# Perceiver block on one core: due times, a load queue and buffer places between attention and FFN

## The chip, the core and the metric

One core of a Trainium2 chip runs the whole program. The metric is device time in microseconds of one execution, as the median of several runs; smaller is better. The engines are named as in the profile: PE is the matrix engine (PEld its weight load), DVE the vector engine, ACT the scalar engine, POOL is GpSimd, SP only issues transfers (SPq its queue).

## What is computed

Four sequences of 128 tokens with 1024 features go through cross attention over four contexts of 2048 tokens (all 8192 context tokens are keys for all queries, with quantised q, k, v and attention), causal self attention with rotary positions, and an FFN whose weights are 4-bit:

```python
x = x + xattn(layernorm(x), ctx, Wq, bq, Wkv, bkv, Wp, bp)     # ... @ Wp + bp
x = x + attn(layernorm(x), Wq, bq, Wk, bk, Wv, bv, Wo, bo)     # ... @ Wo + bo
x = x + ffn(layernorm(x), gate_up_packed, gate_up_scales, down_packed, down_scales)
# ffn: h = silu(x @ Wg.T) * (x @ Wu.T);  y = h @ Wd.T;  y / sqrt(mean(y*y) + 1e-6)
```

## The kernel before

**Split products.** Precise products are made of three passes of a rounded 32-bit type. `split` (L155 to L159) makes of a tensor a high part on ACT (`split_hi`, L155) and on DVE a low part and a difference (`split_lo`, L158 and L159). A product accumulates high times high and low times low into one PSUM tile `acc_a`, and difference times difference into `acc_b`; two DVE operations join them (L1111, L1112). Before it is used, the low part of the activations is scaled on ACT (`scale_low`, L1087).

**The stretch of the change.** After the cross attention the work between attention and FFN is cut into ten halves, `PARTS`, numbered h = 0 to 9: the two column halves of the cross attention's projection Wp (0, 1), the first half of V (2), Q and K halves (3 to 6), the second half of V (7), and the two halves of Wo (8, 9). Each half runs over the four sequences t = 0 to 3, and each of these over eight k-steps of 128 features (`product_step`, L1100; three matmuls of 512 columns a step). Half 0 is a plain product, with its own matmuls (`first_step`, L941) on transposed chunks xoT.

**Weights.** Each half's weights come in four pairs kp = 0 to 3 of 512 KB. `load_pair` (L1028) transfers one into one of two buffers `w_raw`, `split_pair_hi` is its ACT part and `split_pair` its DVE part (tiles sw_h, sw_l, sw_d, six of each). A load waits for the split of the pair two before it. A half's bias goes by `load_bias` (L1018) as a row broadcast to 128 partitions; `add_row` (L1042) adds the row of a projection to the residual x1 on POOL.

**The norm.** After the second half of a projection, for each sequence: join into x1 (`join_residual`), `stats` (L1126), `normalise` (L1131 to L1137, with a root on ACT, L1134) to a tile xn, then `xn_transposes`: eight transposes on PE (L1080), from whose PSUM tiles `pt` (three buffers) the split goes to x3 (tiles x_h, x_l, x_d). Half 1 ends so before V, half 9 before the FFN. For half 1, sequence t's operands come from `first_split` (L1064, L1065) and `first_difference` (L1072), made during half 0.

**Order.** Inside `manual_schedule` the order is written by hand: `do(time, function, ...)` puts a step on an agenda whose times are counted in k-steps, and `perform` records all steps sorted by time (by order of entry where times are equal). Each engine then runs its own instructions in that order, and waits where an operand or buffer is not there. A half starts at `s = PART * h` with PART = 32; sequence t of it ends at `e = s + 8 * t + 8`. Before, the transposes of a norm are due at

```python
do(e + 0.4, normalise, t)
do(e + 7.5, xn_transposes, t)
do(e + 8.35, scale_low, t)
```

The first gate and up product (`first_gate_up`, L1253) is due 12 steps after half 9 and ends the hand order.

**FFN.** There a scheduler orders the instructions. `load_ffn` (L1378) loads 512 KB of weights into one of two buffers fw_raw on SP and splits them (fw_h, fw_l, fw_d); 21 further gate and up pairs follow, then 22 down products. The FFN's tiles take the place of tiles of the stretch before, and an instruction that writes one waits for the last use of whatever lay there. Pools are placed one after the other in the order in which they are opened.

Of the kernel before, what the change touches and what calls it, by code (L numbers as in the profile page):

```python
# [34 lines left out]
F32 = mybir.dt.float32  # L35
# [4 lines left out]
F32R = mybir.dt.float32r  # L40
# [6 lines left out]
P = 128  # L47
B, S, C = 4, 128, 1024
# [23 lines left out]
NI = INNER // P  # L72
# [4 lines left out]
EARLY = 8  # L77
# [9 lines left out]
def tile_perceiver(  # L87
# [26 lines left out]
    nc = tc.nc  # L114
# [29 lines left out]
    def split(src, hi, lo, df):  # L144

        split_hi(src, hi)
        split_lo(src, hi, lo, df)
# [66 lines left out]
    def do(step, fn, *args):  # L219
        agenda.append((step, len(agenda), fn, args))  # L220
# [230 lines left out]
    for t, at in enumerate((4, 10.5, 20, 22.6)):  # L451
# [3 lines left out]
        for n in range(2):  # L455
            at = (10 + 8.15 * t, 42.6 + 7.05 * t)[n]
# [16 lines left out]
    at = 70.8  # L473
# [166 lines left out]
    for s in range(V_AUTO, 2 * KT):  # L640
        at = TILE * s
# [8 lines left out]
    at = TILE * V_AUTO  # L650
# [5 lines left out]
    for s in range(V_AUTO, KT - 2):  # L656
        e = TILE * (s + 1)
# [4 lines left out]
    at = TILE * (KT - 2)  # L662
# [5 lines left out]
    at = TILE * KT  # L668
# [12 lines left out]
    for u in range(KT):  # L681
        at = TILE * (KT + u)
        s = KT + u
# [14 lines left out]
    at = TILE * (KT + 2)  # L698
# [6 lines left out]
    for u in range(first, last):  # L705
        at = TILE * (KT + u)
# [5 lines left out]
    at = TILE * (2 * KT - 1)  # L712
# [21 lines left out]
    with tc.tile_pool(name="at_e", bufs=1) as at_e, tc.tile_pool(  # L734
        name="at_s", bufs=4
    ) as small, tc.tile_pool(name="at", bufs=2) as at, tc.tile_pool(
        name="at_ps", bufs=3, space=PSUM
# [219 lines left out]
        with tc.manual_schedule():  # L957
            for s in range(n_steps + LAG_V):
                n, g = divmod(s, NSC)
# [9 lines left out]
                if n < len(units):  # L969
                    h, t = units[n]  # L970
# [44 lines left out]

    def load_bias(b, n):
        row = sa.tile([P, 512], F32, name="row", tag="row", bufs=3)
        nc.sync.dma_start(out=row, in_=b[ts(n, 512)].partition_broadcast(P))  # L1018
        return row

    def load_pair(h, kp):

        raw = sa_f.tile([P, 2, 512], F32, name="w_raw", tag="w_raw", bufs=2)
        if h < len(PARTS):
            src = w_src2[h][:, 2 * kp : 2 * kp + 2, :]
        else:
            src = gu_d[kp].rearrange("p (two k) n -> p two (k n)", two=2)
        nc.sync.dma_start(out=raw, in_=src)  # L1028
        live["raw", h, kp] = raw

    def split_pair_hi(h, kp):
# [9 lines left out]
    def add_row(t, n, row):  # L1041
        nc.gpsimd.tensor_tensor(x1[:, t, ts(n, 512)], x1[:, t, ts(n, 512)], row, ALU.add)  # L1042
# [107 lines left out]
    def join_values(h, t, n, row):  # L1150
        join(h, t, row[0], vs[n][:, t, :])
# [123 lines left out]
    with tc.manual_schedule():  # L1275
        do(-10, make_causal_mask, nc, mask, -1e30)
        do(-10, last_chunks)
        for step in early_steps[len(FIRST_AT) :]:
            do(-9.4, first_step, *step)
        for n in range(2):  # L1280
            do(-10, keep, ("bp", n), load_bias, xbp, n)
            for t in range(NT):
                do((-9, 15.5)[t // 2] + 8 * n, lambda t, n: add_row(t, n, rows["bp", n]), t, n)
        do(15.4, live["load_x"], 1)

        for h, (w, n) in enumerate(PARTS):
            s = PART * h

            if h > 0:
                for kp in range(NC // 2):  # L1290
                    at = s + {1: (-28, -22, -16, -10), 2: (-37, -33, -6, -3)}.get(h, (-26, -16, -6, -3))[kp]
                    do(at - 9.5, load_pair, h, kp)
                    do(at - 2.5, split_pair_hi, h, kp)
                    do(at + 0.5, split_pair, h, kp)
            if h == 1:
                do(0.6, lambda: nc.sync.dma_start(out=cs, in_=rope.rearrange("i p d -> p i d")))
            bias = {2: abv, 3: abq, 4: abk, 5: abq, 6: abk, 7: abv}.get(h)
            if bias is not None:
                do(s + (-20 if h < 5 else 8 * (17, 21, 25)[h - 5] - s), keep, h, load_bias, bias, n)
            if h in (3, 5):  # L1300
                m = (h - 3) // 2
                do(s + 8, keep, ("bo", m), load_bias, abo, m)
                for t in range(NT):
                    do(s + 9, lambda t, m: add_row(t, m, rows["bo", m]), t, m)
            if h in (2, 7):
                do(s, half_tile, vs, "v", n, f"x{n}")
            for t in range(NT):
                g = s + GROUP * t
                e = g + GROUP
                for k in range(NC):  # L1310
                    if h > 0:
                        do(g + k, product_step, h, t, k)
                    elif t > 1 or k == NC - 1:
                        do(g + k if t > 1 else 14 + t, first_step, t, k)
                if h == 0:
                    if t < 2:
                        e = 15 + t
                        do(14.2 + t, first_split, t)
                    else:
                        do(-9.5 if t == 2 else g - 4.5, first_transposes, t)  # L1320
                        do(g + 1.5, first_split, t)
                    do(PART + (0.05, 3, 9, 15)[t], first_difference, t)
                    do(e + 0.2, join_residual, h, t, n)
                    do(e + 0.3, stats, t, 0)
                elif h == 1:
                    do(e + 0.2, join_residual, h, t, n)
                    do(e + 0.3, stats, t, 1)
                    do(e + 0.4, normalise, t)
                    do(e + 7.5, xn_transposes, t)
                    do(e + 8.35, scale_low, t)  # L1330
                elif h in (2, 7):
                    do(e + 0.2, lambda *a: join_values(*a, [rows[a[0]]]), h, t, n)
                elif h in (3, 5):
                    do(e + 0.2, lambda *a: join_rotary(*a, [rows[a[0]]]), h, t)
                    do(e + 6.5, rotary_transposes, h, t, "qT", 4)
                elif h in (4, 6):
                    do(e + 0.2, lambda *a: join_rotary(*a, [rows[a[0]]]), h, t)
                    do(e + 6.5, rotary_transposes, h, t, "kT", 2)
                    do(e + 9.5, causal_scores, t, n)
                    do(e + 16.6, causal_exponentials, t, n)  # L1340
                    v = e + 24 if n == 0 else e + PART + 2
                    if n == 0 and t == 0:
                        do(v, half_tile, aos, "ao", n, "x2")
                    if n == 1 and t == 0:
                        do(v, half_tile, aos, "ao", n, "x0")
                    for q in range(2):
                        do(v + 0.5 + 2 * q, causal_transposes, t, n, q)
                        do(v + 3.5 + 2 * q, causal_values, t, n, q)
                    if n == 1:
                        do(v + 10.5, ao_transposes, t)  # L1350
                        do(v + 13, scale_low, t)
                else:
                    do(e + 0.2, join_residual, h, t, n)
                    do(e + 0.3, stats, t, n)
                    if n == 1:
                        do(e + 0.4, normalise, t, FP4_UP)
                        do(e + 7.5, xn_transposes, t, True)
                        do(e + 8.35, scale_low, t)
        s = PART * len(PARTS)
        for i in range(2):  # L1360
            at = s - 26 + 10 * i
            do(at - 9.5, load_pair, len(PARTS), i)
            do(at - 2.5, split_pair_hi, len(PARTS), i)
            do(at + 0.5, split_pair, len(PARTS), i)
        do(s + 12, first_gate_up)
        perform()
# [1 line left out]
    opool_s.close()  # L1368


    with tc.tile_pool(name="ff_t", bufs=2) as ff_t, tc.tile_pool(name="ff", bufs=1) as ff:
        hT = [ff.tile([P, 512], F32, name=f"hT{j}", tag=f"hT{j}") for j in range(NI)]
        ss = ff.tile([P, NT, 2], F32, name="ss")

        def load_ffn(src, n):

            raw = ff_t.tile([P, C], F32, name="fw_raw", tag="fw_raw")
            nc.sync.dma_start(out=raw.rearrange("p (i n) -> p i n", n=n), in_=src)  # L1378
            parts = [ff_t.tile([P, C], F32R, name=f"fw_{c}", tag=f"fw_{c}") for c in "hld"]
            split(raw, *parts)  # L1380
            return [t.rearrange("p (i n) -> p i n", n=n) for t in parts]
# [15 lines left out]
        def split_inner(pool, j):  # L1397
            hi, lo = (pool.tile([P, 512], F32R, name=f"h3_{c}{j}") for c in "hl")
            nc.scalar.mul(hi, hT[j], 1.0 - 0.5 / UP)
            nc.vector.tensor_tensor(lo, hT[j], hi, ALU.subtract)  # L1400
            nc.vector.tensor_scalar_mul(lo, lo, UP)
            df = ff.tile([P, 512], F32R, name=f"h3_d{j}", tag=f"hT{j}")
            nc.vector.tensor_tensor(df, hi, lo, ALU.subtract)
            h3[j] = [hi, lo, df]

# [30 lines left out]
        with tc.tile_pool(name="ff_h", bufs=1) as ff_h, tc.tile_pool(  # L1436
            name="y_ps", bufs=1, space=PSUM
# [113 lines left out]
```

## Time and profile before

| | |
|---|---|
| median of 3 runs | 2880.05 us (2878.3 to 2881.0) |
| the profiled execution | 2883.89 us, span 2882.1 us |
| mean granted clock | 0.979 |
| busy, share of the span | PE 93%, DVE 84%, ACT 44%, POOL 16% |
| keys and values, then cross attention | 0 to about 2160 us |
| projection, self attention, Wo (halves 0 to 9) | about 2160 to 2490 us |
| FFN | from about 2490 us |

Times in the profile are microseconds from the span's start. A line of the timeline has start, duration, engine, line, operation, output and inputs, count, and in brackets how long the engine was idle before it and what ended that. "issue" stands where the profile shows no other engine as the cause. A granted clock below 1.00 means that PE ran part of the time at a lower rate. A row of the table of stretches covers the time that its first column names.

### The profile page before, as it was taken

How to read it: one execution, taken by the hardware profiler on the slowest of the kernel's cores; microseconds unless marked ns; L12 is line 12 of the kernel's file. 1: busy time of each engine (PE TensorE's matmuls, PEld its weight loads, DVE VectorE, ACT ScalarE, POOL GpSimd, SP SyncE). 2: the span in 40 equal slices, each digit the busy share in tenths (PEclk: the TensorE clock that was granted, in tenths of full speed). 3: DMA queues.
4: the chain of work that ended last, by engine and by line, in shares of the span. 5: the costliest groups of instructions: out<-in, count | busy, mean ns of one | idle time of the engine just before them, and what ended most of it. 6: DMA issues, size and time to landing. Idle time of an engine off the chain costs nothing.

```text
span 2882.1 us, 41034 instructions
## 1 busy us (share of the span) xinstructions
PE 2666.1 (93%) x15480; PEld 2067.8 (72%) x15480; DVE 2418.6 (84%) x3959; ACT 1266.1 (44%) x1399; POOL 454.6 (16%) x608
## 2 busy tenths in 40 slices
PE   8999999999999999999987877787778899799998
PEld 3788888888888888888864555555555777688876
DVE  6899999555799989898879999999986898676674
ACT  4211212121323333333219999999983245333332
POOL 0011111000012222222122233322311000000000
PEclk9999999999999999999998999999999999899999
DMA  5555565222348777777437788878882322122222
GB/s 186 168 198 199 199 211 211 95 95 95 135 125 205 193 191 186 192 181 198 108 87 162 143 167 163 170 161 154 159 167 87 95 70 67 52 95 92 92 91 91
DMA packets 452711, 413.17 MB, mean 143 GB/s; under 512 B 356953, under 2 KB 361625, under 8 KB 452513
## 3 DMA queue, kind: packets, MB, share of 16 engines
q1 hardware_dynamic: 404928, 252.22, 36.6%
q0 software_dynamic: 46528, 157.29, 17.2%
q8 instruction: 121, 1.98, 0.3%
q10 hardware_dynamic: 1056, 1.05, 0.2%
q14 instruction: 78, 0.63, 0.1%
HBM read 220.14 MB, written 104.34 MB: 113 GB/s over the span
## 4 chain that ended last, share of the span: by engine, by line
PE 71%; DVE 20%; issue 4%; POOL 2%; ACT 1%; DMA 1%; SPq 0%; DVEq 0%; ACTq 0%; POOLq 0%
PE kv_a L342 33%; PE kv_b L342 16%; DVE e L787 13%; PE acc_a L1100 3%; PE y_a L1454 3%; PE gate_a L165 3%; PE up_a L165 3%; POOL sk L760 2%; PE acc_b L1100 2%; PE y_b L1454 1%; PE gate_b L165 1%; PE up_b L165 1%; PE q_ps L292 1%; PE a_pt L830 1%; PE sc L780 1%
## 5 line engine op out<-in xcount | busy, mean ns | idle before, releaser
L342 PE MATMUL kv_a<-w_h,c_h 128*128 128x512 f32 x2048 | 806.3, 394 | 0.0
L342 PE MATMUL kv_a<-w_l,c_l 128*128 128x512 f32 x2048 | 806.0, 394 | 0.2 <-ACT w_l L246 0.2
L342 PE MATMUL kv_b<-w_d,c_d 128*128 128x512 f32 x2048 | 806.0, 394 | 0.0
L787 DVE CUSTOM_DVE_ANT_0 e<-sc,sk 128x1024 f32<-128x1024 f32 x512 | 593.2, 1219 | 8.8 <-PE sc L780 7.7
L815 ACT ACTIVATE a<-e,m,sqs 128x4096 int16<-128x4096 f32 x128 | 486.9, 3804 | 25.2 <-DVE m L804 24.8
L342 PEld LDWEIGHTS kv_a<-w_l,c_l 128*128 128x128 f32 x2048 | 384.8, 188 | 89.6 <-ACT w_l L246 0.6
L342 PEld LDWEIGHTS kv_a<-w_h,c_h 128*128 128x128 f32 x2048 | 384.9, 188 | 88.9 <-issue 0.2
L342 PEld LDWEIGHTS kv_b<-w_d,c_d 128*128 128x128 f32 x2048 | 384.8, 188 | 88.9 <-DVE c_d L159 0.3
L155 ACT ACTIVATE c_h<-c_raw 128x1024 fp32r<-128x1024 f32 x128 | 135.1, 1057 | 415.8 <-PE kv_a L342 413.5
L356 DVE SCALAR_TENSOR_TENSOR f<-kv_a,bkv 128x512 f32<-128x512 f32 x256 | 175.6, 686 | 163.3 <-PE kv_a L342 162.6
L780 PE MATMUL sc<-kt,qT 64*128 64x512 bf16 x1024 | 207.4, 397 | 102.5 <-DVE mx L787 98.5
L581 ACT CAST kst<-kT 128x512 bf16<-128x512 int16 x128 | 89.4, 698 | 309.0 <-DMA kT<-ki 309.0
L830 PE MATMUL a_pt<-ident,a 128*128 128x128 f32 x1024 | 176.5, 297 | 20.7 <-ACT a L815 16.1
L357 DVE SCALAR_TENSOR_TENSOR f<-kv_b,f 128x512 f32<-128x512 f32 x256 | 176.6, 690 | 20.3 <-DVE f L356 0.9
L760 POOL PARTITION_BROADCAST sk<-sk_row x120 | 142.5, 1297 | 312.9 <-DVE mx L787 312.7
L830 PEld LDWEIGHTS a_pt<-ident,a 128*128 128x128 f32 x1024 | 113.0, 146 | 87.2 <-ACT a L815 48.6
L780 PEld LDWEIGHTS <-qT 64*128 64x128 bf16 x1024 | 74.8, 93 | 130.9 <-issue 101.2
L158 DVE TENSOR_TENSOR fw_l<-fw_raw,fw_h 128x1024 fp32r<-128x1024 f32 x64 | 78.2, 1223 | 107.1 <-ACT fw_h L155 106.9
L158 DVE TENSOR_TENSOR c_l<-c_raw,c_h 128x1024 fp32r<-128x1024 f32 x128 | 155.6, 1215 | 6.2 <-ACT c_h L155 5.9
L159 DVE SCALAR_TENSOR_TENSOR c_d<-c_l,c_raw 128x1024 fp32r<-128x1024 f32 x128 | 156.2, 1220 | 2.3
L155 ACT ACTIVATE fw_h<-fw_raw 128x1024 fp32r<-128x1024 f32 x64 | 67.8, 1061 | 179.7 <-PE y_a L1454 75.1
L548 ACT CAST vq<-vi 128x1024 f16<-128x1024 int16 x64 | 66.9, 1046 | 174.2 <-DVE vi L541 128.8
(203 smaller groups left out, 4114.1 us busy)
## 6 DMA issues: line engine op xcount, KB each, us to landing
c_raw<-in_ctxT SPq DMA_DIRECT2D x128, 512.0 KB, 3.6
v_d<-f POOLq DMA_DIRECT2D x64, 512.0 KB, 3.1
vl<-v_d POOLq DMA_DIRECT2D x64, 512.0 KB, 4.2
gu_d<-w_ffn POOLq DMA_DIRECT2D x44, 512.0 KB, 3.1
fw_raw<-gu_d SPq DMA_DIRECT2D x42, 512.0 KB, 3.4
k_d<-kst POOLq DMA_DIRECT2D x128, 128.0 KB, 3.5
vq_d<-vq POOLq DMA_DIRECT2D x32, 512.0 KB, 5.3
kt<-k_d SPq DMA_DIRECT2D x64, 256.0 KB, 3.6
```

Source lines behind the costliest of these rows:

```text
L155: nc.scalar.mul(hi, src, 1.0 - 0.5 / UP)
L158: nc.vector.tensor_tensor(lo, src, hi, ALU.subtract)
L159: nc.vector.scalar_tensor_tensor(df, lo, -1.0 - UP, src, ALU.mult, ALU.add)
L165: nc.tensor.matmul(ps, lhsT=lhs(i, k), rhs=rhs(i, k), start=(k == 0 and i != 1), stop=(k == NC - 1 and i != 0),)
L342: nc.tensor.matmul(ps, lhsT=tokens[s][i][:, k, :], rhs=w3[s < KT][k][i][:, ts(n, 512)], start=(k == 0 and i != 1), stop=(k == NC - 1 and i ...
L356: nc.vector.scalar_tensor_tensor(f, a, 1.0 + 1.0 / UP, bias[s < KT][n], ALU.mult, ALU.add)
L357: nc.vector.scalar_tensor_tensor(f, b, -1.0 / UP, f, ALU.mult, ALU.add)
L760: nc.gpsimd.partition_broadcast(tile_of_scales(h, g), sks_at[h][32 * c : 32 * c + 1, ts(half, SC)], channels=P)
L780: nc.tensor.matmul(ps[:, ts(i, 512)], lhsT=qT[rows, h, ts(t, P)], rhs=kts[h, g // 2][rows, ts(g % 2, 512)], start=True, stop=True,)
L787: nc.vector.tensor_tensor_reduce(out=state[n]["e"][-1][:, ts(g % (NSC // NEC), SC)], in0=ps, in1=sks_at[h, g], scale=1.0, scalar=LOWEST, o ...
L815: nc.scalar.activation(a, st["e"][c], AF.Exp, bias=st["m"], scale=sqs[:, 0, t, h : h + 1], accum_out=sums[h][:, t, c : c + 1],)
L830: nc.tensor.transpose(pt[:, i, :], a[:, at_word + P * i : at_word + P * i + P], ident)
```

## The change

It changes four things, and no operation. First, due times: the transposes after half 1 go from e + 7.5 to e + 9.5, behind two k-steps of the next sequence; after half 9 they go to e + 9.5 for sequences 0 and 1, e + 8.6 for 2, and stay for 3, so that the norm of sequence 3 comes ahead of the split of sequence 2. Second, the weight pairs of half 1 get other due times. Third, the two rows of the bias bp and the pairs 0 and 1 of half 1 are issued on GpSimd's queue instead of SP's. Fourth, the FFN's raw buffers get a pool of their own, behind a new pool of the first ten hT tiles, so that fw_raw lies where bias rows and an xn buffer were (before, it lay where values of the attention were), and fw_h, fw_l and fw_d move down by 8 KB a partition.

```diff
     def load_bias(b, n):
         row = sa.tile([P, 512], F32, name="row", tag="row", bufs=3)
-        nc.sync.dma_start(out=row, in_=b[ts(n, 512)].partition_broadcast(P))
+        queue = nc.gpsimd if b is xbp else nc.sync
+        queue.dma_start(out=row, in_=b[ts(n, 512)].partition_broadcast(P))
...
     def load_pair(h, kp):
...
-        nc.sync.dma_start(out=raw, in_=src)
+        queue = nc.gpsimd if (h, kp // 2) == (1, 0) else nc.sync
+        queue.dma_start(out=raw, in_=src)
...
-                    at = s + {1: (-28, -22, -16, -10), 2: (-37, -33, -6, -3)}.get(h, (-26, -16, -6, -3))[kp]
+                    at = s + {1: (-28, -24, -12, -7), 2: (-37, -31, -6, -3)}.get(h, (-26, -16, -6, -3))[kp]
                     do(at - 9.5, load_pair, h, kp)
                     do(at - 2.5, split_pair_hi, h, kp)
                     do(at + 0.5, split_pair, h, kp)
...
                     do(e + 0.4, normalise, t)
-                    do(e + 7.5, xn_transposes, t)
-                    do(e + 8.35, scale_low, t)
+                    do(e + 9.5, xn_transposes, t)
+                    do(e + 10.4, scale_low, t)
...
                         do(e + 0.4, normalise, t, FP4_UP)
-                        do(e + 7.5, xn_transposes, t, True)
-                        do(e + 8.35, scale_low, t)
+                        do(e + (9.5, 9.5, 8.6, 7.5)[t], xn_transposes, t, True)
+                        do(e + (10.4, 10.4, 8.7, 8.35)[t], scale_low, t)
...
-    with tc.tile_pool(name="ff_t", bufs=2) as ff_t, tc.tile_pool(name="ff", bufs=1) as ff:
-        hT = [ff.tile([P, 512], F32, name=f"hT{j}", tag=f"hT{j}") for j in range(NI)]
+    with tc.tile_pool(name="ff_t", bufs=2) as ff_t, tc.tile_pool(
+        name="ff_a", bufs=1
+    ) as ff_a, tc.tile_pool(name="ff_raw", bufs=2) as ff_raw, tc.tile_pool(name="ff", bufs=1) as ff:
+        inner_pool = [ff_a if j < EARLY + 2 else ff for j in range(NI)]
+        hT = [inner_pool[j].tile([P, 512], F32, name=f"hT{j}", tag=f"hT{j}") for j in range(NI)]
...
         def load_ffn(src, n):
-            raw = ff_t.tile([P, C], F32, name="fw_raw", tag="fw_raw")
+            raw = ff_raw.tile([P, C], F32, name="fw_raw", tag="fw_raw")
...
-            df = ff.tile([P, 512], F32R, name=f"h3_d{j}", tag=f"hT{j}")
+            df = inner_pool[j].tile([P, 512], F32R, name=f"h3_d{j}", tag=f"hT{j}")
```

## The prediction

> **What bounds the kernel now.** I read the table of stretches first, then the waits of TensorE, then the timelines of the three places where it stands. Columns of the stretches: busy time of PE, PEld, DVE, ACT and POOL (instructions in brackets), granted clock, DMA share, GB/s.
>
> ```profile
> 2155.00:2160.00 5.00, 4.10 (x58) 2.86 (x53) 1.63 (x4) 0.00 (x0) 0.00 (x0) 1.00 1.12 322
> 2160.00:2165.00 5.00, 4.11 (x54) 2.62 (x55) 0.59 (x2) 0.00 (x0) 0.00 (x0) 1.00 1.05 241
> ...
> 2174.00:2212.00 38.00, 28.25 (x76) 15.87 (x75) 27.89 (x30) 14.48 (x16) 6.83 (x5) 0.82 0.36 117
> 2212.00:2264.00 52.00, 44.73 (x196) 35.87 (x195) 40.37 (x58) 15.33 (x21) 0.00 (x0) 0.93 0.16 47
> ...
> 2452.00:2509.00 57.00, 41.81 (x179) 33.22 (x178) 37.92 (x59) 16.95 (x24) 0.00 (x0) 0.85 0.17 56
> 2509.00:2690.00 181.00, 181.00 (x777) 145.61 (x778) 126.87 (x151) 65.64 (x90) 0.00 (x0) 1.00 0.28 90
> ```
>
> The FFN (last row) keeps PE busy throughout, so nothing is to be won there. In the 147 us of the three stretches that the change touches, PE stands 32 us and its clock falls to 0.82 to 0.93.
>
> Place A, the first output projection (timelines of ACT, DVE, PE and the SP queue):
>
> ```profile
> 2119.96 40.57 SPq L845 DMA_TRANSPOSE aT_d<-a  x8
> 2160.88 0.81 SPq L1018 DMA_DIRECT2D row<-in_xbp  x2
> ...
> 2176.54 1.06 ACT L155 ACTIVATE sw_h<-w_raw 128x1024 fp32r<-128x1024 f32 x1 [5.75 <-DMA w_raw<-in_xWp]
> 2177.50 1.04 ACT L155 ACTIVATE x_h<-x 128x1024 fp32r<-128x1024 f32 x1
> 2179.72 0.68 DVE L1117 TENSOR_TENSOR x<-acc_a,x 128x512 f32<-128x512 f32 x1
> 2180.50 5.38 PE L941 MATMUL acc_a<-wp,xoT 128*128 128x512 f32 x8 [5.54 <-issue]
> ```
>
> ACT waits 5.75 us for the third weight pair with the x_h of sequence 0, which needs nothing from it, queued behind. DVE's join (L1117) comes behind that, and PE waits for the accumulator that the join frees. Place B is the norm of half 1, place C that of half 9 and the door of the FFN:
>
> ```profile
> 2205.22 3.78 PE L1100 MATMUL acc_b<-sw_d,x_d 128*128 128x512 f32 x8 [4.21 <-DVE x_d L1072]
> 2242.74 1.94 PE L1080 MATMUL pt<-ident,xn 128*128 128x128 f32 x8 [4.68 <-DVE xn L1137]
> 2484.03 1.95 PE L1080 MATMUL pt<-ident,xn 128*128 128x128 f32 x8 [6.01 <-DVE xn L1137]
> 2492.44 1.95 PE L1080 MATMUL pt<-ident,xn 128*128 128x128 f32 x8 [6.46 <-DVE xn L1137]
> ...
> 2478.34 1.23 DVE L158 TENSOR_TENSOR fw_l<-fw_raw,fw_h 128x1024 fp32r<-128x1024 f32 x1
> 2479.60 1.17 DVE L158 TENSOR_TENSOR fw_l<-fw_raw,fw_h 128x1024 fp32r<-128x1024 f32 x1
> 2480.75 1.22 DVE L159 SCALAR_TENSOR_TENSOR fw_d<-fw_l,fw_raw 128x1024 fp32r<-128x1024 f32 x1
> 2481.95 1.21 DVE L159 SCALAR_TENSOR_TENSOR fw_d<-fw_l,fw_raw 128x1024 fp32r<-128x1024 f32 x1
> 2483.08 0.81 DVE L1137 TENSOR_SCALAR xn<-x,ln_mv,ln_rstd 128x1024 f32<-128x1024 f32 x1
> ```
>
> PE waits for the normalised xn, and at C DVE spends 4.8 us on splits of FFN weights in the middle of the norm of sequence 2. After a stand over 4 us the eight transposes take 1.95 us instead of 1.05: each long gap costs a slow clock on top.
>
> **The change part by part.** No instruction is added or removed; what changes is order, queue and addresses. The sum is made against the profiled execution (2883.89 us, span 2882.1, 1.8 us around it), which lies 3.84 us above the median of 2880.05.
>
> *Place A, order.* With the new due times ACT splits the third pair after the x_h of sequences 0, 1 and 2. ACT ends the first two sw_h at 2170.8, so x_h of sequence 0 no longer waits; DVE is busy with the two first splits until 2174.95 (2169.87 and four ops), then x_l and the join: 2174.95 + 1.15 + 0.7 = 2176.8 against 2180.4, 3.6 us earlier. But a new wait comes: DVE has the x_l of sequence 3 ahead of the fourth pair's split, and its x_h stands on ACT behind the sw_h of the next half's first pair, whose load starts only when the third pair's split frees its buffer. That split falls at 2184.9 and meets the four GpSimd adds, which follow the x load and so come 3.6 us earlier too (2185.5 to 2191.4). Under such adds the same two ops took 2.36 and 2.17 us (2191.58, 2193.97) instead of 1.21 and 1.23. So the split ends at 2189.1, the load (about 3.9 us) lands at 2193.0, sw_h and x_h take 1.0 each to 2195.0, and DVE, idle from 2190.5, does x_l 1.2, two splits 4.8 and x_d 1.2: 2202.2 against 2205.16. A gains 3.0 (4.4 if the adds miss the split).
>
> *Place A, the GpSimd queue.* Four issues leave SP: two rows of 256 KB and two pairs of 512 KB. SP is held by transposes until 2160.88; GpSimd is free at 2154.2, and its queue is mask, rows, two adds, two pairs, two adds, x load. Rows issued at 2155 land at 2161.3 (5.9 us, the row of SP's) to 2164 (8.7, the 1 MB loads of this queue); two adds 2.5; an issue 0.75; landing 3.1 (v_d of this queue) to 4.4 (SP's w_raw): the first pair is there at 2169.0 at best by the slower landing and at 2171.7 at worst, and ACT wants it at 2168.77. Nothing is won, since ACT is held till then by copies that wait for PE (2166.84); up to 3.0 us may be lost, and I take 0 beyond the next term, near the lower end because the adds' cover (ACT's copies) moves with it. That term: the DMA engines are full (1.12 and 1.05) with the last transposes, for which PE waits (av on aT_d, 1.78 us before 2160.89), and 0.52 MB of rows now go among them; at 382 GB/s, the rate of 2150 to 2155, 1.4 us. Bounds 0 and 2.2 (241 GB/s); I take 1.4. A: -3.0 + 1.4 = -1.6, bounds -4.4 and 0 (late pairs and full DMA engines hit the same start, so they don't add).
>
> The Trainium skill speaks against this edit: "DMA: Bandwidth & Descriptors", section "Issuing engines are not separate DMA queues", says that DMAs of all issuing engines interleave on the same 16 engines and that a second issuer saves only sequencer time, usually small. Here that sequencer time is not small (SP stood in transposes for 40 us), but by the rule the edit can only cost and the sum is the one with the 1.4; by the SP row alone the cost would be 0 and the sum -17.0.
>
> *Place B.* PE now does two k-steps of the next sequence before the transposes, and DVE norms the next sequence before it splits the last. Let X be the end of the x_d of sequence 0 (2205.2 before). DVE from X: join of sequence 3 and stats 1.4, split 2.4, x_d 1.2 = X+5.0; norm 3.85 (2219.45 to 2223.3) X+8.9; two x_d 2.4; norm 1, X+15.1; split of transposes 2.65, 17.7; norm 2, 21.6; split 24.2; two weight splits 29.1; norm 3, 33.0; split 35.6; weight 38.1; join v 39.5; split 42.2; join v 43.6. DVE is thus the pace and no faster: the last x_d before was at 2247.6 = X+42.4. What goes is PE's standing: half 2 of sequence 1 starts at X+30.5 and not behind a 4.68 us gap with slow clock, with gaps of 1.1 and 1.3 left (after 1.29 us gaps the trace shows matmuls at full pace, 0.23 us apart). Sequence 2 starts at X+39.6 on the freed accumulator, 3 at X+45.2, end X+50.8 against 2263.2 = X+58.0. DVE follows: the last join v at X+53.9, a weight split that waits for its load until X+55.3, the first f at X+57.8 against 2269.70 = X+64.5. I take the later engine: -6.7. Bounds: -10.3 (PE's gaps of 7.3 after X and some 3 of slow clock) and -3.8 (only the DVE idle of 2.35 and 1.44 that the order itself closes).
>
> Halves 3 to 8 shift as a block: PE is busy 48.45 of 50 us from 2310, and the row loads, GpSimd adds and weight loads follow buffers that come free earlier.
>
> *Place C.* Same order, and the FFN's raw buffers now lie over the bias rows and the buffer of the last xn, so their loads wait for the last transposes. The four fw splits thus leave the norm. By the same durations, from the join at 2458.37: norm 0 to 2462.3; norm 1 (PE done 2463.4) to 2467.3; weight split 2469.6; split 2472.2; norm 2 to 2476.05; split 2478.7; norm 3 to 2482.55; split 2485.15. PE ends its last k-step at 2476.7, transposes 2 at once and 3 at 2482.6 to 2484.9 (slow clock). ACT's x_h of sequence 3 stands behind the scaling of 2 (2486.25), its first half ends 2486.9, and the first gate matmul starts there instead of 2494.22: -7.3. The FFN loads start at 2484.9 instead of 2473.63, land by 2488.7, are split by 2495.6 and wanted at 2500.1: 4.5 us of cover, and what lies beyond it costs its full length. Bounds: -4.8 (the fw splits alone) and -9.1 (the first 16 gate matmuls, 5.69, at the 3.90 of the next 16).
>
> Sum: -1.6 - 6.7 - 7.3 = -15.6: 2868.3 for a profiled run, 2864.5 for the median. All bounds together: -23.8 to -8.6.
>
> **The rivals.** (1) Only C pays: DVE, 47.77 of 50 us busy from 2310, sets the pace and gives A and B back in the rotary halves. For it: B's DVE end is no earlier; against: PE waits there only four times, 8.5 us. 2880.05 - 7.3 = 2872.8. (2) No change: A and B are given back as in (1), and the FFN's first loads land 11.8 us late (4.5 covered, 7.3 lost; the median landing of fw_raw is 3.4): 2880. (3) Slower: GpSimd's chain of rows, adds and weight issues makes the pairs late, and ACT stands at sw_h with every x_h behind it, one for one. From a lateness of 15.6 us it eats all, from 21.4 it is slower by over 0.2%; at 23 us, 2887. Against: the worst row gives 3.0.
>
> **How the numbers follow.** Forecast 0.66, (1) 0.20, (2) 0.08, (3) 0.06. 0.2% is 5.8 us, about what a measurement of this kernel tells from no change. Forecast and (1) are faster: 0.86, less 0.01 for an edge of (1). The forecast's bounds give 2856.3 to 2871.5; with (1) included and the extreme end shaved, 2857 to 2874.
>
> **What would show it.** Right: ACT's x_h<-x at about 2171 to 2172 after two sw_h; GpSimd's w_raw issues between 2163 and 2168; x_d of sequence 0 near 2203; no 4.68 us gap in half 2; fw_l after the last x_d; x3's first gate matmul 14 to 17 us earlier. Wrong: sw_h waiting for w_raw for over 3 us at A, a gap of PE at gate 1 of over 1.5 us, or a DVE stand in place of the PE stands.

## The result and the profile after

| | before | after |
|---|---|---|
| median of 12 runs of each, run together | 2880.07 us | 2877.13 us |
| ratio after to before, 95% interval | | 0.9992 (0.9984 to 1.0000) |
| the profiled execution | 2883.89 us, span 2882.1 | 2877.45 us, span 2875.6 |
| mean granted clock | 0.979 | 0.981 |

By the ratio and the medians 2 to 3 us were won, with an interval that reaches to none, and not 15.6. By the bound of the prediction that is no change. Three places moved, in two directions. (The functions of the changed kernel stand three lines lower, later FFN code more.)

The table of stretches of the kernel after, with the columns and stretches of before:

```profile
2155.00:2160.00 5.00, 4.46 (x61) 3.11 (x59) 1.63 (x4) 0.00 (x0) 0.84 (x2) 1.00 1.10 351
2160.00:2165.00 5.00, 0.11 (x3) 0.11 (x4) 0.00 (x0) 0.00 (x0) 0.11 (x1) 0.90 1.22 163
2174.00:2212.00 38.00, 30.70 (x90) 16.34 (x89) 26.29 (x25) 17.68 (x21) 7.28 (x5) 0.91 0.33 104
2212.00:2264.00 52.00, 48.95 (x215) 38.30 (x214) 45.15 (x66) 14.85 (x22) 0.00 (x0) 0.97 0.20 66
2452.00:2509.00 57.00, 48.43 (x208) 38.34 (x207) 42.07 (x65) 19.36 (x28) 0.00 (x0) 0.91 0.16 56
2509.00:2690.00 181.00, 181.00 (x777) 145.63 (x776) 128.05 (x152) 64.37 (x89) 0.00 (x0) 1.00 0.27 93
```

The three stretches that the change was to tighten are tighter: PE is busy 128.1 of 147 us there, 114.8 before. But from 2160 to 2165 PE does almost nothing (0.11 us, 4.11 before), while the DMA engines are over-full (1.22) and move less (163 GB/s, 241 before). Place A in the timelines of the kernel after:

```profile
2150.31 14.23 SPq L845 DMA_TRANSPOSE aT_d<-a  x2
...
2154.70 1.15 POOL L1019 DMA_DIRECT2D row<-in_xbp  x2
...
2164.89 1.03 PE L858 MATMUL av<-vq,aT_d 128*128 128x64 f16 x16 [5.43 <-DMA aT_d<-a]
...
2166.16 2.05 PE L941 MATMUL acc_a<-wp,x 128*128 128x512 f32 x2
...
2175.62 2.01 ACT L155 ACTIVATE sw_h<-w_raw 128x1024 fp32r<-128x1024 f32 x2
...
2177.52 1.05 ACT L155 ACTIVATE x_h<-x 128x1024 fp32r<-128x1024 f32 x1
...
2183.43 3.67 PE L941 MATMUL acc_a<-wp,xoT 128*128 128x512 f32 x8 [1.63 <-issue]
...
2198.96 1.06 ACT L155 ACTIVATE sw_h<-w_raw 128x1024 fp32r<-128x1024 f32 x1 [5.68 <-DMA w_raw<-in_aWv]
```

The rows go out on GpSimd at 2154.70, the last transposes land at 2164.9, and PE waits 5.43 us for them (1.78 before). The matmuls behind that stand run at half pace (2.05 us for two, 1.10 before). The order part works as forecast: x_h follows the two sw_h at once, and the gap of 5.54 us with slow clock at the third sequence is 1.63 without. But all of it is late. Places B and C:

```profile
2208.20 3.76 PE L1103 MATMUL acc_b<-sw_d,x_d 128*128 128x512 f32 x8 [3.83 <-DVE x_d L1075]
...
2241.19 0.63 PE L1083 MATMUL pt<-ident,xn 128*128 128x128 f32 x4 [1.32 <-DVE xn L1140]
...
2275.80 1.09 PE L1180 MATMUL pt<-ident,f 128*128 128x128 f32 x4 [4.61 <-DVE f L1174]
...
2482.99 1.09 PE L1083 MATMUL pt<-ident,xn 128*128 128x128 f32 x4 [4.48 <-DVE xn L1140]
...
2487.17 6.04 PE L1256 MATMUL acc_a<-x_h,sw_h 128*128 128x512 f32 x16 [1.78 <-ACT x_h L155]
```

At B the gap of 4.68 us is 1.32, but the one at the first rotary transposes has grown from 2.91 to 4.61. At C the two gaps of 6.01 and 6.46 us have become one of 4.48, and the first gate matmul starts at 2487.17, 7.05 us earlier.

### The profile page after: what moved, and what is told of

Same layout as the page of the kernel before. It is cut to its first block, busy times and chain, and to the rows that moved or that the text cites. A ratio compares the mean times of both kernels' runs of the same rounds, so it can differ in the third digit from the quotient of the medians.

```text
span 2875.6 us, 41060 instructions
## 1 busy us (share of the span) xinstructions
PE 2666.2 (93%) x15480; PEld 2066.7 (72%) x15480; DVE 2420.0 (84%) x3959; ACT 1264.5 (44%) x1399; POOL 459.7 (16%) x612
## 4 chain that ended last, share of the span: by engine, by line
PE 70%; DVE 21%; issue 4%; POOL 2%; DMA 2%; ACT 1%; SPq 0%; DVEq 0%; ACTq 0%; POOLq 0%
PE kv_a L342 32%; PE kv_b L342 16%; DVE e L787 13%; PE y_a L1462 3%; PE gate_a L165 3%; PE up_a L165 3%; PE acc_a L1103 3%; POOL sk L760 2%; PE q_ps L292 2%; PE up_b L165 1%; PE gate_b L165 1%; PE y_b L1462 1%; PE acc_b L1103 1%; PE a_pt L830 1%; DVE sw_l L158 1%
```

## The experiments

The theory was that the rows on GpSimd's queue go among the last transposes and cost more than A and B gain. The rivals were that the late start was chance or not the queue's, and that the rotary halves give back what comes early. Ratios are to the kernel before, run alongside, with 95% intervals; 0.0010 is 2.9 us. Since the cross attention before the change, whose instructions are the same in all, ends at different times in different profiles (2151.1 to 2157.7), the steps below are counted from the end of its last exponential. "Step 1" is PE's start on the last aT_d, "step 2" its start on the xo transposes, X the end of the x_d of sequence 0, J the first join of half 9 (its second operation), G the FFN's first matmul of gate pair 1.

### The queue edits

**Both taken back (a_sp).**

```diff
-        queue = nc.gpsimd if b is xbp else nc.sync
-        queue.dma_start(out=row, ...)
+        nc.sync.dma_start(out=row, ...)
...
-        queue = nc.gpsimd if (h, kp // 2) == (1, 0) else nc.sync
-        queue.dma_start(out=raw, in_=src)
+        nc.sync.dma_start(out=raw, in_=src)
```

> The changed kernel with both queue edits taken back: the two bias rows and the pairs 0 and 1 of half 1 go on SP's queue again, behind the last DMA transposes; everything else stays as in the change. Theory 1 (the rows that GpSimd issues at 2154.7 share the DMA engines with the last transposes, and aT_d lands late): PE's last wait for aT_d falls back from 5.43 us to under 2.5, PE reaches the xo transposes 5 to 7 us earlier (2173.7 to about 2167), the x_d of sequence 0 ends at 2202 to 2203, and the median falls by 5 to 7 us against the changed kernel, to about 2870 to 2872, ratio to the kernel before 0.9965 to 0.9975. Theory 2 (the late start is not due to the queue, or is only a matter of this one profiled execution): the wait for aT_d stays at 4 us or more and the median within 1.5 us of 2877. Theory 3 (the rotary halves give back what comes earlier, since DVE paces them): the wait falls as in theory 1 but the join of half 9 starts at 2454 as before and the median stays within 1.5 us of 2877.

Measured: 2866.15 us, ratio 0.9961 (0.9948 to 0.9974). PE of this kernel:

```profile
2159.65 0.64 PE L858 MATMUL av<-vq,aT_d 128*128 128x64 f16 x16 [1.82 <-DMA aT_d<-a]
...
2160.36 1.10 PE L941 MATMUL acc_a<-wp,x 128*128 128x512 f32 x2
```

The wait is that of before and the clock stays full. Step 1 comes 3.85 us earlier than in the kernel after (6.96 against 10.81), step 2 6.69 us earlier, X 6.71 us (47.36 against 54.07). So of the 6.7 us 3.9 are the late landing and 2.8 the slow clock behind it; nothing is made up between step 2 and X. The rival that all is given back falls: the median is 11 us below that of the kernel after (9 by the ratios), more than the 5 to 7 expected. The rival of chance falls too, with the profiles of all runs: step 1 is at 10.25 to 13.41 in the four kernels with both rows on GpSimd's queue, and at 5.87 to 7.44 in the eleven with both on SP's.

**The other way round: the kernel before with both queue edits alone (b_queue).** The diff is the reverse of the one above.

> The kernel before with only the two queue edits. Theory 1 (rows among the transposes): PE waits for aT_d 4 to 6 us (1.78 before), reaches the xo transposes at 2172 to 2174 (2166.84 before), and the median is 4 to 7 us above the kernel before, ratio 1.0014 to 1.0024. Theory 2 (the queue edit is harmless): the wait stays under 2.5 us and the ratio is within 0.0007 of 1. Theory 3 (rotary halves give back whatever shifts): start late as in theory 1, but the join of half 9 no later than before and the ratio within 0.0007 of 1.

Measured: 2889.78 us, ratio 1.0034 (1.0022 to 1.0047), some 10 us slower, more than expected. Step 1 is at 10.25 (6.7 to 7.4 in the six kernels with before's order of loads and the loads on SP), step 2 at 17.53 (12.6 to 15.0):

```profile
2167.85 1.04 PE L858 MATMUL av<-vq,aT_d 128*128 128x64 f16 x16 [4.98 <-DMA aT_d<-a]
```

At X 4.2 of the 10 us are there (54.86, against 50.7 as the mean of the six); no run shows where the rest arises.

**Rows back on SP, pairs on GpSimd (a_rows_sp), and pairs back, rows on GpSimd (a_pairs_sp).** Each takes back one half of the diff above.

> The changed kernel with only the two bias rows back on SP's queue; the pairs 0 and 1 of half 1 stay on GpSimd's queue, between its adds, which wait for the rows. Theory 1 (the rows among the transposes cost): PE's wait for aT_d falls under 2.5 us as with both edits taken back. But the rows land at about 2166, the first two adds take 2.5 us, so the first pair is issued at about 2169 and lands at 2173 to 2174, where ACT would want it at about 2169: ACT stands 4 to 5 us at sw_h. The median lies between, 2872 to 2877. Theory 2 (not the queue): wait for aT_d as in the changed kernel, 4 us or more, median 2877 or above.

> The changed kernel with the two pairs of half 1 back on SP's queue; only the two bias rows stay on GpSimd's. Theory 1 (the rows among the transposes are what costs; the pairs matter only where they would be late): PE's aT_d wait starts 10 to 11 us after the end of the exponentials as in the change, the pairs land before ACT comes to them, and the median is that of the change, 2876 to 2879. Rival (the pairs behind GpSimd's adds are what costs, as the 6.9 us between the two kernels with rows on SP would say): the median falls to 2870 to 2873.

Measured: 2873.03 us, ratio 0.9979 (0.9971 to 0.9987), and 2877.67 us, ratio 0.9993 (0.9983 to 1.0002). With the rows on SP step 1 is at 5.89; the pairs are issued behind GpSimd's adds, and ACT stands 3.37 us at sw_h (4 to 5 expected). With the rows on GpSimd step 1 is at 11.09 and the time is that of the kernel after, pairs on SP or not. So the rows carry the cost; the pairs cost something only where the rows don't.

**Less and more among the transposes (a_one_row, a_pairs_early).** One row on GpSimd; or the two pairs due at -10, right behind the rows:

```diff
-        queue = nc.gpsimd if b is xbp else nc.sync
+        queue = nc.gpsimd if b is xbp and n == 0 else nc.sync
```
```diff
-                    do(at - 9.5, load_pair, h, kp)
+                    do(-10 if (h, kp // 2) == (1, 0) else at - 9.5, load_pair, h, kp)
```

> The changed kernel with the second of the two bias rows back on SP's queue, so that 0.26 MB instead of 0.52 MB go among the last DMA transposes; pairs as in the change. Theory 1a (bytes: the transposes are late in proportion to what goes among them): PE's last wait for aT_d starts some 2 us earlier than in the change, counted from the last exponentials of the cross attention: 8.5 to 9.2 us after their end, where the change has 10.8 and the kernels with both rows on SP 5.9 to 7.3. Theory 1b (any load from that queue at that time costs the whole delay): 10.3 to 11.3 us. Theory 1c (only the second row, which starts among the very last transposes, costs): under 7.5 us.

> The changed kernel with the two pairs of half 1 issued on GpSimd's queue right behind the two rows, ahead of its adds, so that 1.57 MB instead of 0.52 MB go out at the time of the last DMA transposes. Theory 1a (bytes in the DMA engines): 0.52 MB cost 3.5 to 4.9 us, so 1.05 MB more cost another 3 (at 382 GB/s, the rate just before) to 8 us: PE's aT_d wait starts 14 to 19 us after the end of the exponentials (10.8 in the change) and the median rises by 2 to 8 us, to 2879 to 2885. Theory 1b (a matter of issue and order, not of bytes: the pairs were late because they stood behind the adds): the start stays at 10 to 11.5 us, the pairs are there early and the median falls by 1 to 3 us.

Measured: step 1 at 8.66 with 0.26 MB (one run, 2876.53 us), 10.81 with 0.52 MB, and 13.41 with 1.57 MB (2878.98 us, ratio 1.0000, 0.9988 to 1.0013). PE's waits in the two:

```profile
2166.14 1.04 PE L858 MATMUL av<-vq,aT_d 128*128 128x64 f16 x16 [3.46 <-DMA aT_d<-a]
```
```profile
2168.41 1.03 PE L858 MATMUL av<-vq,aT_d 128*128 128x64 f16 x16 [8.21 <-DMA aT_d<-a]
```

The delay grows with what goes out there: 1.7 us for the first row, 2.2 for the second (from 6.96), 2.6 for the two pairs, where I expected 3 at least.

**The same rows at the same time, issued by ACT (a_rows_act).** Pairs on SP.

```diff
-        queue = nc.gpsimd if b is xbp else nc.sync
+        queue = nc.scalar if b is xbp else nc.sync
...
-            do(-10, keep, ("bp", n), load_bias, xbp, n)
+            do(-10.5, keep, ("bp", n), load_bias, xbp, n)
```

> The changed kernel with the pairs on SP's queue and the two bias rows issued by ACT right behind its last exponentials, that is at the time at which GpSimd issues them in the change. Theory (time and bytes: the rows share the DMA engines with the last transposes, whoever issues them): PE's aT_d wait starts 9.5 to 11.5 us after the end of the exponentials, as with GpSimd, and the median is 2875 to 2879. Rival (GpSimd's own queue is what delays the transposes): the start comes at 5.9 to 7.5 us, as with SP, and the median is 2864 to 2869.

Measured: neither. Step 1 is at 8.58, 2871.76 us, ratio 0.9978 (0.9966 to 0.9990). By ACT's queue the same 0.52 MB cost 1.6 us of landing, by GpSimd's 3.9 (4.1 with the pairs on SP, as here). PE's wait:

```profile
2161.09 1.03 PE L858 MATMUL av<-vq,aT_d 128*128 128x64 f16 x16 [3.03 <-DMA aT_d<-a]
```

The views of the DMA queues show what differs: packets, MB and share of the engines by queue (q1 are SP's transposes, q0 is GpSimd's queue, q10 ACT's), from the end of the last exponential to the landing of the last transposes. First the kernel after, 2154.08 to 2164.55; then the kernel with both edits taken back, 2152.69 to 2159.29; then the rows by ACT, 2152.51 to 2160.7:

```profile
q0 software_dynamic: 600, 2.20, 61.0%
q1 hardware_dynamic: 2421, 0.61, 53.5%
```
```profile
q0 software_dynamic: 424, 1.61, 61.5%
q1 hardware_dynamic: 2539, 0.64, 49.2%
```
```profile
q0 software_dynamic: 434, 1.65, 53.0%
q1 hardware_dynamic: 2330, 0.59, 34.8%
q10 hardware_dynamic: 288, 0.52, 21.7%
```

Share times length is the time that the packets took on the 16 engines. By ACT the rows add 1.8 us, and the transposes keep their pace, 0.020 us a packet on one engine, as without rows (0.020). By GpSimd its own packets take 6.4 us instead of 4.1, and the transposes' take 5.6 instead of 3.2, though they are no more: 0.037 us each. By the same reckoning they took 0.033 to 0.037 us in all four kernels with both rows on GpSimd's queue, 0.027 with one row, and 0.019 to 0.023 in the eleven with the rows on SP. So the rows add 1.8 to 2.3 us of packets, and what is beyond that in the 3.9 is transposes whose packets take longer. Two shorter windows of the kernel after, 2153 to 2159 and 2162 to 2163, and 2158 to 2159 of the kernel with both edits taken back:

```profile
q0 software_dynamic: 565, 2.17, 98.4%
q1 hardware_dynamic: 516, 0.13, 10.7%
```
```profile
q1 hardware_dynamic: 238, 0.06, 121.0%
q0 software_dynamic: 5, 0.02, 4.2%
```
```profile
q1 hardware_dynamic: 1151, 0.29, 127.8%
```

While GpSimd's queue has packets of 4 KB to move, the transposes' 256-byte packets get about as many turns and a sixteenth of the bytes: 516 in 6 us, 86 in a us. Alone they go at 1151 in a us. In all kernels GpSimd's queue is busy there with its 1 MB loads of wp and x, and the rows keep it running longer. These turns say who goes first; the packets to be moved stay the same. The added time lies behind them: from 2162 to 2163 GpSimd's queue has 5 packets left, and yet the transposes move only 238 with the engines' share at 121.0%. Why their packets take longer behind rows from that queue is not shown; only the issuer, the amount and the time were varied.

### The order and the pools

**A's order alone, and B's alone (b_pairs_due, b_norm1, b_norm1_again),** on the kernel before:

```diff
-... {1: (-28, -22, -16, -10), 2: (-37, -33, -6, -3)}
+... {1: (-28, -24, -12, -7), 2: (-37, -31, -6, -3)}
```
```diff
-                    do(e + 7.5, xn_transposes, t)
-                    do(e + 8.35, scale_low, t)
+                    do(e + 9.5, xn_transposes, t)
+                    do(e + 10.4, scale_low, t)
```

> The kernel before with only the new due times of the weight pairs of halves 1 and 2 (place A's order alone, all loads on SP). By the prediction's place A: x_h of sequence 0 no longer stands behind a sw_h that waits for its load, the join of sequence 0 comes 3.6 us earlier and x_d of sequence 0 3 us earlier, PE's gap of 5.54 us at the third sequence of half 0 shrinks to about 1.7 us with no slow clock after it. Theory 1 (gains at A stay): ratio 0.998 to 0.9995 (-1.5 to -5 us). Rival (the rotary halves give A back, DVE being the pace): the same trace at A, and a ratio within 0.0005 of 1.

> The kernel before with only the new due times of half 1's transposes (place B alone). By the prediction: the PE gap of 4.68 us with its slow clock goes, the last join of half 2 comes 6.7 us earlier counted from the x_d of sequence 0, ratio 0.9977. Theory 1 (half of that, as the trace of the changed kernel has it: DVE stands 2 us for a sw_h that ACT has behind the scaling of sequence 2): ratio 0.9985 to 0.9993 (-2 to -4.5 us). Rival (rotary halves give it back): 4.68 us gap gone, last join of half 2 2 to 4 us earlier, but the first join of half 9 as before and the ratio within 0.0005 of 1.

> Place B alone once more, with more rounds. Theory (given back): ratio 0.9993 to 1.0000. Rival (half of the forecast stays): 0.9983 to 0.9990. In both, first f join some 5 us earlier counted from the x_d of sequence 0 than in the kernels with the old order (62.7 to 64.5).

Measured: A 2880.18 us, ratio 0.9994 (0.9983 to 1.0004), which is inconclusive by time alone. Its trace is as forecast: the gap of 5.54 us is 1.61, and X is at 47.47, where six kernels with the old order and all loads on SP have 49.2 to 52.5. B: 0.9988 (0.9978 to 0.9999), as if half stayed, and again 0.9996 (0.9987 to 1.0006), as if it were given back. Counted from X, these are the first f joins of the four rotary halves and J; old is the mean of four kernels (before and those of place C below), new that of the two:

| from X | half 3 | half 4 | half 5 | half 6 | J |
|---|---|---|---|---|---|
| old | 63.3 | 92.8 | 128.7 | 158.4 | 250.2 |
| new | 57.7 | 89.2 | 125.6 | 156.9 | 249.2 |
| gain | 5.6 | 3.6 | 3.1 | 1.5 | 1.0 |

The 5.6 us at the first f join are nearly the 6.7 of the forecast, and four fifths are gone at half 9. The 1.0 that is left there is less than the spread of the four old kernels (248.5 to 254.0). Where they go first, in the timeline of PE of B alone:

```profile
2267.19 1.08 PE L1177 MATMUL pt<-ident,f 128*128 128x128 f32 x4 [4.94 <-DVE f L1171]
```

PE is there earlier, but DVE has four rotary operations on f still to do, and PE's order has nothing else ahead of the transposes.

**B taken out of the kernel without queue edits (a_sp_no_b):** the same lines, the other way.

> The kernel with both queue edits taken back (ratio 0.9961), and half 1's transposes back at their old due times: places A and C without B. Theory (B is given back in the rotary halves, where PE and DVE are both nearly full): first f join 3 to 5 us later counted from the x_d of sequence 0, first join of half 9 at most 1.5 us later, ratio 0.9958 to 0.9968. Rival (B keeps half of what was forecast): first join of half 9 3 to 4 us later, ratio 0.9971 to 0.9977.

Measured: 2869.82 us, ratio 0.9975 (0.9966 to 0.9984), against 0.9961 with B; J from X 252.5, against 248.1. Both fit the rival that half stays, not the theory, but the intervals overlap, and in these two profiles the slow clock between X and J lasted 15.4 us against 10.1, which at half rate is 2.6 of the 4.4 us. Together: B is worth 1 to 4 us, and the intervals don't settle it closer.

**Place C: both parts, due times alone, pools alone (c_both, c_due, c_pool),** on the kernel before, with the change's own lines.

> The kernel before with only what bears on place C: the due times of half 9's transposes and the FFN's pools. By the prediction's place C: first gate matmul 7 us earlier (2494.2 to about 2487), ratio 0.9974 to 0.9977 (-6.5 to -7.5 us), places A and B as before. If what C gains is lost later in the FFN, the first gate matmul is 7 us earlier and the ratio is 0.999 or above.

> The kernel before with only the due times of half 9's transposes. The four splits of FFN weights (4.8 us) stay in the middle of the norm on DVE. By the prediction's place C: -7.3 us for both parts, of which the splits are 4.8; so this part gives about -2.5 us, ratio 0.999, first gate matmul 2 to 3 us earlier relative to half 9's first join. If the order is what counts, more: -5 to -7.

> The kernel before with only the FFN's pools as in the change. The four splits of FFN weights leave the norm: by the prediction's lower bound of place C about -4.8 us, ratio 0.9983, the two PE gaps of 6.0 and 6.5 us shrink. If the pool alone gives nothing without the new order, the ratio is within 0.0005 of 1 and the gaps stay.

Measured: 0.9977 (0.9968 to 0.9987), 0.9987 (0.9978 to 0.9996), 0.9979 (0.9969 to 0.9990). From J to G: 49.7 before, 42.3 with both, 46.2 with the due times, 45.8 with the pools. So 7.3 us, 3.5 and 3.9: in the traces they add up, and 4.8 for the pools was too much, 2.5 for the due times too little. With the pools alone the gap of 6.01 us shrinks to 2.08, but that of 6.46 stays (6.52); with the due times alone they are 3.62 and 4.07.

**One step further (a_sp_xh3).** In the kernel with both queue edits taken back, the wait for the first pair of half 2 still has x_h of sequence 3 behind it (5.60 us).

```diff
-2: (-37, -31, -6, -3)
+2: (-35.9, -31, -6, -3)
```

> The kernel with both queue edits taken back, and the first pair of half 2 due 1.1 steps later (-35.9 for -37), so that ACT makes x_h of sequence 3 ahead of the sw_h that waits 5.6 us for its load. Theory (DVE is the chain from there on): DVE's stand of 4.75 us at x_l of sequence 3 goes, x_d of sequence 0 ends 43 to 44.5 us after the end of the exponentials (47.4 without), PE's gap of 3.83 us at the first acc_b shrinks below 1, and the median falls by another 2 to 4.5 us, to 2861.5 to 2864. Rival (PE or the rotary halves give it back): x_d earlier as above, but half 9's first join and the median as without (2866, within 1.5 us).

Measured: 2865.84 us, ratio 0.9950 (0.9938 to 0.9963), the best of all; X at 43.43 (47.36), J at 291.94 (295.45). Timelines of DVE and PE:

```profile
2187.93 2.19 DVE L1064 TENSOR_TENSOR x_l<-xoT,x_h 128x1024 fp32r<-128x1024 f32 x1
...
2190.05 2.30 DVE L158 TENSOR_TENSOR sw_l<-w_raw,sw_h 128x1024 fp32r<-128x1024 f32 x1
...
2197.20 1.16 PE L1100 MATMUL acc_b<-sw_d,x_d 128*128 128x512 f32 x2 [2.60 <-DVE x_d L1072]
```

DVE's stand is gone, though its operations now lie beside GpSimd's adds and take 2.2 us instead of 1.23; PE still waits 2.60 us, and I had expected less than 1. The median hardly differs from the 2866.15 of the kernel without it (2861.5 to 2864 expected); by the ratios it is 3 us better, with overlapping intervals.

## Why the prediction was wrong

- **A's order (-3.0): held at X.** X is at 47.5 with A's order alone, against 50.7 as the mean of the six kernels with the old order: 3.2 us. By time it is 1.7, with an interval that takes in none. The new wait that was forecast, x_l of sequence 3 behind the load of the next half's first pair, is there: ACT stood 5.68 us, DVE 4.83.
- **The rows among the transposes (+1.4, bounds 0 to 2.2): this step failed.** Measured 3.9 us of landing and 2.8 us of slow clock, 6.7 at X; by the runs of both directions the queue edits cost some 9 to 10 us (0.9961 to 0.9992, and 1.0034). I priced the rows' bytes by a mean rate and took the transposes' own time as given. By ACT's queue that comes out: 1.6, close to my 1.4. By GpSimd's the transposes' packets themselves took 0.037 us instead of 0.020, 2.4 us in all; why stays open. I had also reckoned with a slow clock behind the gaps taken away and with none behind a gap made. Beyond X the profile of the kernel after loses another 3.3 us to J (251.4 against 248.1); its clock was slow there for 17.3 us against 10.1, which at half rate is 3.6. How much of that is due to the change and how much to chance stays open.
- **Late pairs (0): held** as long as the rows are there too; without them 3.4 us of standing at ACT, where my upper bound was 3.0.
- **B (-6.7): right at the first f join** (57.7 from X with B alone, where I had said 57.8; 59.9 in the kernel after; DVE's stand of 2.07 us for a sw_h that ACT has behind the scaling of sequence 2 is in both, so it doesn't make that difference), **wrong in "halves 3 to 8 shift as a block".** From there DVE and PE take turns in pacing: PE's gap at the first rotary transposes grows by up to 2 us, and 1 to 4 us are left. That is the mechanism of rival (1), for B alone. This is the second step that failed: B's term was -6.7, and -1 to -4 were measured.
- **C (-7.3): held.** From half 9's first join to gate pair 1 it is 7.1 us less in the kernel after, 7.3 by itself; the first FFN loads came in time and the FFN was as busy as before.
- **Rival (3), slower by GpSimd's chain:** wrong in the place. The pairs were not what came late in the kernel after, but the queue edits alone do make the kernel slower by 0.34%.

The terms with the measured ones: -3.2 to -1.7 for A's order, -1 to -4 for B, -7 for C, +9 to +10 for the queue: between -5 and 0, and -2.3 by the ratio. Taking the queue edits back gives 0.9961, 11 us; my sum without their term, -17.0, would have been 6 us too good; B's shortfall of 3 to 6 is in that.

The rule of the Trainium skill that I weighed, "DMA: Bandwidth & Descriptors", section "Issuing engines are not separate DMA queues", had the right sign: these transfers do run on the same engines as the transposes. Its other half, that who issues saves only sequencer time, is not what was measured here: the same rows at about the same time cost 1.6 us of landing by ACT and 3.9 by GpSimd.

## What to carry to other kernels

A load that is moved to an idle queue to go out earlier must be priced against what the DMA engines are doing at that time: look for a transfer for which someone waits, and read in the DMA views how long the packets of each queue take with the load and without it. Its bytes alone gave 1.4 us here, and 3.9 were measured by one queue and 1.6 by another. A gap that an edit makes can cost a slow clock behind it, as a gap taken away can save one. Where two engines are both over 95% busy, as PE and DVE are here from 2310 to 2360, time won ahead of them is worth what is left of it at the end of that stretch, so read a landmark there before counting it.

## What was not expected of the hardware

- Packets of 256 bytes beside a queue of 4 KB packets: 86 in a us; alone: 1151. Behind the two rows on GpSimd's queue each of them took 0.037 us on an engine, behind the same rows on ACT's 0.020.
- The same gap gives a slow clock in one run and none in another. At the rotary transposes near 2395 PE stands 2.73 us in most kernels, and the stretch behind it has a granted clock of 0.66 before and after, and of 1.00 with place C alone and with the queue edits taken back:

```profile
2395.00:2400.00 5.00, 4.96 (x25) 3.74 (x27) 4.90 (x7) 2.99 (x14) 0.00 (x0) 0.66 0.00 0
```
```profile
2385.00:2391.00 6.00, 5.54 (x39) 4.47 (x40) 5.87 (x8) 3.58 (x16) 0.00 (x0) 1.00 0.00 1
```

The first is the kernel after, the second the one with the queue edits taken back (its times are some 10 us earlier). In all profiles the slow stretches, but for the one at the end of the run, last 3.41 us or a multiple of it. The Trainium skill, "TensorE: Matmul & The Clock Gate", section "What's actually happening", has a free-running window of 3413 ns, which fits the length and the chance; the stand of 2.73 us, behind which the slow stretch begins in some profiles, is shorter than the idle window it names. From X to J the slow stretches add up to 10 to 20 us in different profiles, at half rate 5 us of difference at most, and J - X differs by as much (248.1 to 254.0): single profiles of this kernel can't tell gains of that size there.
